# Depthwise-convolution images kept in device memory, and two pieces' results taken up behind the next scans

## The chip, the cores and the metric

The kernel runs on one core of one Trainium2 chip. The core has a matrix engine (TensorE, PE in the profile; its weight loads are listed apart as PEld), a vector engine (VectorE, DVE), a scalar engine (ScalarE, ACT), GpSimd (POOL) and SyncE (SP), which in this program does nothing but issue transfers. Each engine works through its own list of instructions in order, and waits on semaphores for the others. Sixteen DMA engines move what the queues hand them. The metric is device time in microseconds (us) of one execution, the median of several. All times here are microseconds unless another unit is named.

## What is computed

The program is a network of four layers on x of 4 images, 128 channels, 64×64 pixels. Only layers 0 and 1 are touched by the change. Cut to what matters, and with the group normalisation `_gn` over 32 groups of channels:

```python
x = x + conv_mamba(_gn(x), ...)     # layer 0
x = x + conv3x3(_gn(x), ...)        # layer 1, a full 3x3 convolution of 128 channels
# layers 2 and 3: attention and experts on the tokens (t = to_tokens(x)), not touched

def conv_mamba(x):                  # layer 0, for every image
    feat = gelu(dwconv2d(x, conv1_w, conv1_b))          # depthwise 3x3, zero padding
    ca = sigmoid(relu(feat.mean((2, 3)) @ ca1_w.T) @ ca2_w.T)
    feat = gelu(dwconv2d(feat * ca, conv2_w, conv2_b))  # depthwise 3x3
    scores = 0.7 * sigmoid(head(feat)) + 0.3 * sigmoid(10 * var_over_channels(x))
    order = argsort(-mean of scores over 4x4 patches)   # 256 patches are ranked
    x1n = layernorm(x in that order + pe in that order) # 4096 tokens of 128 channels
    xm, z = split(x1n @ in_proj_w.T)                    # 256 + 256
    xc = silu(conv1d(xm))                               # causal, 4 taps
    dt_low, B, C = split(xc @ x_proj_w.T)               # 8, 16, 16
    dt = softplus(dt_low @ dt_proj_w.T + dt_proj_b)
    # a scan over 4096 tokens, for 256 channels and 16 states
    h = exp(dt * A) * h + dt * B * xc ;  y = sum_s(h * C)
    y = (y + D * xc) * silu(z)
    return (y @ out_proj_w.T) put back by the inverse order
```

## The kernel before

Layers 0 and 1 are one function, `layers01` (from line 235). Its main loop is `scan` (line 544): the four images' sequences, 4096 tokens each, run one after the other in 8 chunks of 512 tokens, and each chunk in 8 groups of two states. A group has one product on VectorE (L683, `hs = dtx * b_ps`, 128×2048), four decays on ScalarE (L686, an Exp into PSUM, two buffers), four scans on VectorE (L687, `tensor_tensor_scan`), a copy of the last state (L690) and two products with C on GpSimd (L693), and eight matmuls on TensorE, one (`b_ps`, one PSUM buffer) that spreads B over the partitions for the next group and the rest (`y_ps`) that sums the states; `hs` has three buffers. There are 256 such groups. A chunk's inputs are prepared a step per group by the generator `enter` during the chunk before: xc, the gate z, dbc, dt, and then eight SP transfers (L624) that copy dt and dtx into the scan's layout (dt2, dtx2). The two rows of C are read back from a scratch array `c_d` in device memory, spread over partitions by two SP transfers per group (L656, `c_sb`, three buffers).

What else the layers need is done beside the scans, in pieces. `others(b)` is a generator of the work beside sequence b: `end(b-1)`, which puts the finished sequence back into its image, runs layer 1's convolution on it and stores it (`put_back`, `convolve`; the store is L755), and then `in_order(b+1)`, which prepares the next image: the load (L333), the group normalisation (`groupnorm_padded`: bn_stats at L135, the normalised and zero-padded image `xp` of 66×66 at L174), the two depthwise convolutions, the ranking, the permutation. Each `yield` of these generators names a cost; after every group the loop at the end of `scan` takes pieces until their costs reach what is due by then. What is due follows from COST_END, COST_ORDER and the table ROOM (a share for each group of a chunk). `in_order(0)` has no scans to run beside and runs alone at the start, and `end(3)` alone at the end.

A piece's matmuls are issued when it is taken; what takes their results up (an activation or a copy) is put in a list with `later(...)`, and `K.flush()` issues what the list holds. The loop flushes before every piece it takes:

```python
while done < due:
    K.flush()
    done += next(beside, due)
```

TensorE's order is the order in which this Python code issues (a manual schedule for PE alone). For the other engines' queues a scheduler sets the order by its own estimate of when each instruction can run. So an instruction that must wait can stand in a queue ahead of another that could go.

A depthwise convolution is done on TensorE: for each of 8 row blocks of the image, `gather` (L350 to L359) builds a tile `under` of 96 partitions, which are three row shifts of 32 channels, for each of the four channel groups; 12 matmuls (`convolved`, three column shifts by four groups; the trace counts 24) then make the convolution. `under` has two buffers. The source is the padded image in on-chip memory, xp for the first convolution and fp, the first one's gelu, for the second; a gather is 12 transfers of 66 KB, all issued by SP at L355. Per image there are 16 gathers, so 192 transfers.

Of the kernel before, what the change touches and what calls it, by code (L numbers as in the profile page):

```python
# [17 lines left out]
P = 128  # L18
NB = 4
HW = 64  # L20
# [9 lines left out]
class Common:  # L30
# [98 lines left out]
    def groupnorm_padded(self, xb, xp, small, psum):  # L129


        nc = self.nc
        st = small.tile([P, NCH, 6], F32, name="gn_st")
        for c in range(NCH):
            nc.vector.bn_stats(st[:, c, :], xb[:, c * CH : (c + 1) * CH])  # L135
            if c % 2:
                yield 1
        mv = small.tile([P, 2], F32, name="gn_mv")
        nc.vector.bn_aggr(mv, st)
        nc.gpsimd.memset(xp[:, 0, :], 0.0)  # L140
        nc.gpsimd.memset(xp[:, HW + 1, :], 0.0)
        nc.gpsimd.memset(xp[:, 1 : HW + 1, 0:1], 0.0)
        nc.gpsimd.memset(xp[:, 1 : HW + 1, HW + 1 : HW + 2], 0.0)
        yield 4
        mp = psum.tile([P, 1], F32, name="gn_mp", tag="mm")
        self.mm(mp, self.group_mean, mv[:, 0:1])
        gm = small.tile([P, 1], F32, name="gn_gm")
        v2 = small.tile([P, 1], F32, name="gn_v2")

        def variance():  # L150
            nc.vector.tensor_copy(gm, mp)
            d = small.tile([P, 1], F32, name="gn_d")
            nc.vector.tensor_tensor(d, mv[:, 0:1], gm, ALU.subtract)
            nc.vector.scalar_tensor_tensor(v2, d, d, mv[:, 1:2], ALU.mult, ALU.add)

        self.late.append(variance)
        yield 4
        yield 4
        vp = psum.tile([P, 1], F32, name="gn_vp", tag="mm")
        self.mm(vp, self.group_mean, v2)  # L160
        rs = small.tile([P, 1], F32, name="gn_rs")
        off = small.tile([P, 1], F32, name="gn_off")

        def scale():
            sd = small.tile([P, 1], F32, name="gn_sd")
            nc.scalar.activation(sd, vp, AF.Sqrt, bias=self.eps5)
            nc.vector.reciprocal(rs, sd)
            nc.vector.scalar_tensor_tensor(off, gm, -1.0, rs, ALU.mult, ALU.mult)

        self.late.append(scale)  # L170
        yield 4
        yield 4
        for c in range(NCH):
            nc.scalar.activation(  # L174
                xp[:, 1 + 8 * c : 9 + 8 * c, 1 : HW + 1],
                xb[:, c * CH : (c + 1) * CH].rearrange("p (y x) -> p y x", x=HW),
                AF.Identity,
                bias=off,
                scale=rs,
            )  # L180
            if c % 2:
                yield 1
# [52 lines left out]
def layers01(K, xd, dpool, w, w1):  # L235
# [4 lines left out]
    DS = 16  # L240
    NQ, NG = 4, DS // 2

    COST_END, COST_ORDER = 127.2, 215.2
    ROOM = (0.04, 0.04, 0.09, 0.21, 0.41, 0.61, 0.81, 1.0)
    with ExitStack() as ctx:
        pool = lambda name, bufs, **kw: ctx.enter_context(tc.tile_pool(name=name, bufs=bufs, **kw))
        cst = pool("l0_const", 1)
# [41 lines left out]
        spread = cst.tile([32, DS, 64], F32, name="spread")  # L289
        nc.vector.tensor_copy(spread, state.unsqueeze(2).to_broadcast([32, DS, 64]))  # L290
        c_d = dpool.tile([2, DS, CH], F32, name="c_d")

        pair = cst.tile([P, 64], F32, name="pair")
        nc.vector.tensor_tensor(pair, K.ident[:, 0:64], K.ident[:, 64:128], ALU.add)
# [41 lines left out]
        def in_order(b, made, work, psum):  # L336
# [10 lines left out]
            nc.gpsimd.memset(fp[:, 1 : HW + 1, HW + 1 : HW + 2], 0.0)  # L347
            fsum = small.tile([P, NCH], F32, name="fsum")

            def gather(img, c):  # L350

                t = work.tile([96, 4, 8 * (HW + 2)], F32, name="under", bufs=2)
                for ky in range(3):
                    for g in range(4):
                        nc.sync.dma_start(  # L355
                            out=t[32 * ky : 32 * ky + 32, g],
                            in_=img[32 * g : 32 * g + 32, 8 * c + ky : 8 * c + ky + 8, :].rearrange("p y x -> p (y x)"),
                        )
                return t  # L359

            def convolved(under, taps):
# [10 lines left out]
                        )  # L372
                return ps

            under = gather(xp, 0)
            yield 4
            unders = [under, gather(xp, 1)]
            for c in range(NCH):
                ps = convolved(unders.pop(0), deep1)
                later(  # L380
                    nc.scalar.activation,
                    fp[:, 1 + 8 * c : 9 + 8 * c, 1 : HW + 1],
                    ps.rearrange("p (y x) -> p y x", x=HW),
                    AF.Gelu,
                    bias=conv1_b,
                    accum_out=fsum[:, c : c + 1],
                )
                if c + 2 < NCH:
                    unders.append(gather(xp, c + 2))
                yield 5  # L390
            favg = small.tile([P, 1], F32, name="favg")
            nc.vector.tensor_reduce(favg, fsum, AX.X, ALU.add)
            nc.vector.tensor_scalar(favg, favg, 1.0 / L, None, ALU.mult)
            unders = [gather(fp, 0), gather(fp, 1)]
            yield 4
            c1p = psum.tile([32, 1], F32, name="c1p", tag="mm")
            mm(c1p, ca1_wT, favg)
            c1 = small.tile([32, 1], F32, name="c1")
            later(nc.scalar.activation, c1, c1p, AF.Relu)
            yield 4  # L400
            c2p = psum.tile([P, 1], F32, name="c2p", tag="mm")
            mm(c2p, ca2_wT, c1)
            ca = small.tile([P, 1], F32, name="ca")
            later(nc.scalar.activation, ca, c2p, AF.Sigmoid)
            yield 2

            sm = small.tile([P, 256], F32, name="sm")
            for c in range(NCH):  # L410
# [8 lines left out]
                f2 = work.tile([P, CH], F32, name="f2", tag="ln_xc")  # L419
                later(nc.scalar.activation, f2, ps, AF.Gelu, bias=conv2_b, scale=ca)  # L420
                if c + 2 < NCH:
                    unders.append(gather(fp, c + 2))
                yield 5
                vp = psum.tile([P, CH], F32, name="pv_var", tag="mm")
                mm(vp, K.var1, sq)
                pv = work.tile([P, CH], F32, name="pv")
                later(nc.scalar.activation, pv, vp, AF.Tanh, scale=5.0)
                yield 1.2
                hp = psum.tile([P, CH], F32, name="head", tag="mm")
                mm(hp, head_bc, f2)  # L430
                sc = work.tile([P, CH], F32, name="sc")
                later(nc.scalar.activation, sc, hp, AF.Tanh, bias=head_b, scale=0.5)
                yield 1.2
                nc.vector.scalar_tensor_tensor(sc, pv, 3.0 / 7.0, sc, ALU.mult, ALU.add)
                nc.vector.tensor_reduce(
                    sm[:, 32 * c : 32 * c + 32].rearrange("p (a b) -> p a b", b=16),
# [45 lines left out]
            for c in range(NCH):  # L482
# [14 lines left out]
                later(nc.scalar.activation, sq, mp, AF.Square)  # L497
                later(nc.scalar.copy, xl, mp)
                yield 1.2
                vp = psum.tile([P, CH], F32, name="pos_var", tag="mm")  # L500
                mm(vp, K.mean, sq)

# [9 lines left out]

                K.late.append(normed)
                yield 1.2
                for a in range(2):
                    nc.scalar.activation(
                        xn[:, :, 16 * (2 * c + a) : 16 * (2 * c + a) + 16].rearrange("p (y x) b -> p y b x", x=4),
                        xl[:, a * 256 : (a + 1) * 256].rearrange("p (y b x) -> p y b x", y=4, x=4),
                        AF.Identity,
                        bias=norm_b,  # L520
                        scale=norm_g,
                    )
# [6 lines left out]
            for o in range(0, 16, 2):  # L529
                tp = psum.tile([P, 4, P], F32, name="perm_t", tag="mm")  # L530
                for j in range(4):
                    h = j % 2
                    nc.tensor.transpose(tp[:, j, :], xn[:, o + j // 2, h * P : (h + 1) * P], K.ident)
                ts = work.tile([P, 4, P], F32, name="perm_s", tag="pv")
                later(nc.vector.tensor_copy, ts, tp)
                yield 1.2
                pp = psum.tile([P, 2, 256], F32, name="perm_p", tag="mm")
# [3 lines left out]
                yield 2.2  # L541
            made.append((xq, perm_inv))

        def scan(seqs, others, work, psum, psbc, psex, psy):
# [127 lines left out]
            for n, (b, c) in enumerate(chunks):  # L672
# [7 lines left out]
                for g in range(NG):  # L680
# [24 lines left out]
                    if g > 0:  # L705
                        next(leaving, None)
                    next(coming, None)
                    while done < due:
                        K.flush()
                        done += next(beside, due)  # L710
                    if past is not None:
                        add(*past)
                        if g == 0:
                            leaving = leave(past[0])
                            next(leaving)
# [6 lines left out]
        def put_back(xb, om, perm_inv, prep, psum):  # L722
# [3 lines left out]
            for o in range(0, 16, 2):  # L726
# [4 lines left out]
                ts = prep.tile([P, 4, P], F32, name="perm_s", tag="pv")  # L731
                later(nc.scalar.copy, ts, tp)
                yield 1.2
                pp = psum.tile([P, 2, 256], F32, name="perm_p", tag="mm")
                for j in range(4):
                    mm(pp[:, j // 2, :], ts[:, j, :], perm_inv[j % 2], start=j % 2 == 0, stop=j % 2 == 1)
                for j in range(2):
# [3 lines left out]
                        nc.vector.tensor_tensor, at, at, pp[:, j, :].rearrange("p (a b) -> p a b", b=16), ALU.add  # L741
                    )
                yield 2.2

        def convolve(b, xb, psum):

# [2 lines left out]
            for c in range(2 * NCH):  # L749
# [2 lines left out]
                at = xb[:, c * CH // 2 : (c + 1) * CH // 2]  # L752
                later(nc.vector.scalar_tensor_tensor, at, ps, bias, at, ALU.add, ALU.add)
                yield 4.5
            nc.sync.dma_start(out=xd[b], in_=xb)  # L755

        def end(b, seq, work, psum):
# [1001 lines left out]
```

## Time and profile before

| | us |
|---|---|
| median of 3 runs | 10960.34 (10960.1 to 10969.78) |
| the profiled execution, its own time | 10954.31 |
| its span in the trace | 10952.5 |
| stage 1, `in_order(0)` alone | 0 to 276 |
| scans of sequences 0 to 3, with the work beside them | 276 to 3069 |
| `end(3)` alone | 3069 to 3250 |
| layers 2 and 3 | 3250 to 10952 |

Times of the eight chunks of the scans, from the starts of the products of L683 (a chunk is eight groups; the last chunk of sequence 3 is counted to the start of its last group):

| sequence | chunks 0 to 7, us |
|---|---|
| 0 | 67.7, 92.9, 85.9, 78.7, 79.9, 105.7, 89.6, 72.6 |
| 1 | 90.1, 82.0, 105.5, 95.7, 90.2, 84.3, 143.0, 80.3 |
| 2 | 90.3, 81.9, 105.7, 95.2, 87.7, 84.1, 142.8, 79.9 |
| 3 | 75.9, 75.8, 80.1, 71.5, 69.1, 69.7, 69.5, 47.1 |

How it is read. A page of the profile has the busy time of each engine, and groups of instructions by line and operation: how many, their busy time, the mean of one, and the idle time of the engine just before them with what ended it. A line of the waits view reads "engine, what waited <- what released it: total us, times, longest". A line of a timeline reads "start, us, engine, line, operation, output<-input, shapes, count, [idle before <- releaser]". SPq is SP's queue of issues; the time of such a line is the time of issuing, not of moving the data. Idle time of an engine that the rest does not wait for costs nothing, so an engine's share of busy time alone does not say what a change is worth. A line such as L328 or L90 is that of a helper (`later` and `mm`), and the tile's name says which step it is.

### The profile page before, as it was taken

Reading aid. Unit: us, or ns where it says so; the run is one execution under the profiler, and the core shown is the slowest. Engines: PE = TensorE matmul, PEld = TensorE weight load, DVE = VectorE, ACT = ScalarE, POOL = GpSimd, SP = SyncE. Lnnn points to the kernel's source line nnn. Section 1 sums busy time; section 2 is a strip of 40 time slices with the busy share of each in tenths; the row PEclk is TensorE's granted clock in tenths of the full one; section 3 lists DMA queues with packets and bytes.
Section 4 is the critical chain, followed back from the end, with each engine's and each line's share of the span. In section 5 each row is a group of like instructions: output and inputs, shape, how many; then the busy total and the mean of one; then the engine's idle time right before and its main releaser. Section 6 shows DMA issues by size and latency. Waiting matters only on the chain. (4 is left out here: it accounts for less than half of the span.)

```text
span 10952.5 us, 184078 instructions
## 1 busy us (share of the span) xinstructions
PE 9041.6 (83%) x71952; PEld 3464.4 (32%) x71952; DVE 7656.5 (70%) x8462; ACT 7514.8 (69%) x10319; POOL 5233.6 (48%) x3143
## 2 busy tenths in 40 slices
PE   5777778777857999968999968999969999966767
PEld 2223323222332333323333323333323333323333
DVE  2788668668846777757777757777757777744563
ACT  2666565665527999958999948999948999932431
POOL 1565555556624666535665535665535655620000
PEclk8788878877878999979999979999979999977888
DMA  3322322322212222121221222212222212123004
GB/s 83 87 67 57 90 69 56 99 59 59 70 52 40 38 32 34 32 78 35 37 33 33 32 78 38 33 34 33 32 79 39 33 33 34 30 88 96 14 16 139
DMA packets 524327, 581.59 MB, mean 53 GB/s; under 512 B 106233, under 2 KB 329537, under 8 KB 520897
## 3 DMA queue, kind: packets, MB, share of 16 engines
q1 hardware_dynamic: 523456, 569.81, 22.6%
q8 instruction: 568, 9.31, 0.4%
q14 instruction: 303, 2.47, 0.1%
HBM read 373.96 MB, written 76.55 MB: 41 GB/s over the span
## 5 line engine op out<-in xcount | busy, mean ns | idle before, releaser
L1204 ACT ACTIVATE ex<-score 128x1024 f32<-128x1024 f32 x5120 | 4932.2, 1032 | 471.0 <-PE score L90 180.8
L90 PE MATMUL ctx_ps<-ex,qt 128*32 128x512 f32 x20480 | 2719.1, 595 | 0.0
L1151 POOL TENSOR_TENSOR folded<-ex 128x1024 f32<-128x1024 f32 x704 | 1679.4, 2386 | 2073.6 <-ACT ex L1204 2062.0
L1210 DVE STREAM_TRANSPOSE turned<-ex 128x1024 f32<-128x1024 f32 x1536 | 1879.5, 1224 | 470.1 <-ACT ex L1204 426.9
L90 PE MATMUL acc_ps<-turned,turned_v 128*32 128x256 f32 x24576 | 1826.3, 388 | 180.2 <-DVE turned L1190 177.4
L1190 DVE STREAM_TRANSPOSE turned<-ex 128x1024 f32<-128x1024 f32 x1536 | 1854.0, 1207 | 0.0
L90 PE MATMUL score<-queries,keys 32*128 32x512 f32 x10240 | 1359.9, 496 | 120.5 <-ACT ex L1204 74.3
L687 DVE TENSOR_TENSOR_SCAN hs<-decay,carry,hs 128x512 f32<-128x512 f32 x1024 | 1253.0, 1266 | 200.3 <-ACT decay L686 186.0
L686 ACT ACTIVATE decay<-dt,a_neg 128x512 f32<-128x512 f32 x1024 | 701.0, 689 | 788.0 <-DVE hs L687 764.3
L693 POOL TENSOR_TENSOR hs<-hs,c_sb 128x1024 f32<-128x1024 f32 x512 | 1204.9, 2374 | 46.1 <-DMA c_sb<-c_d 26.7
L90 PEld LDWEIGHTS score<-queries,keys 32*128 32x128 f32 x10240 | 524.7, 182 | 2176.5 <-issue 1664.1
L1152 POOL TENSOR_TENSOR quarters<-folded 128x512 f32<-128x512 f32 x704 | 905.1, 1286 | 55.2
L90 PEld LDWEIGHTS acc_ps<-turned,turned_v 128*32 128x32 f32 x24576 | 562.1, 108 | 897.0 <-issue 556.0
L90 PEld LDWEIGHTS ctx_ps<-ex,qt 128*32 128x32 f32 x20480 | 684.0, 110 | 461.0 <-DVE ctx L1133 53.2
L683 DVE TENSOR_TENSOR hs<-dtx,b_ps 128x2048 f32<-128x2048 f32 x256 | 582.2, 2274 | 256.6 <-PE b_ps L90 173.4
L90 PE MATMUL y_ps<-hs,pair 128*64 128x512 f32 x2048 | 644.2, 752 | 137.3 <-POOL hs L693 137.2
L1133 DVE COPY ctx<-ctx_ps 128x512 f32<-128x512 f32 x256 | 177.0, 691 | 669.6 <-PE ctx_ps L90 663.2
L690 POOL COPY carry<-hs 128x4 f32<-128x4 f32 x256 | 59.3, 232 | 1019.7 <-DVE hs L687 976.8
L1023 POOL TENSOR_TENSOR turned_v<-v,quarter 128x1024 f32<-128x1024 f32 x192 | 459.2, 2392 | 18.1 <-DMA v<-value_d 18.1
L1197 DVE TENSOR_REDUCE dacc<-quarters 128x2 f32<-128x512 f32 x704 | 453.4, 644 | 8.0 <-POOL quarters L1152 8.0
L90 PE MATMUL ln_var<-ln_sq,mean 128*128 128x512 f32 x384 | 240.2, 710 | 182.9 <-ACT ln_sq L105 158.1
L90 PE MATMUL b_ps<-dbc,spread 32*128 32x512 f32 x512 | 319.4, 706 | 70.7 <-DVE hs L683 70.7
(353 smaller groups left out, 9684.3 us busy)
## 6 DMA issues: line engine op xcount, KB each, us to landing
c_sb<-c_d SPq DMA_DIRECT2D x512, 128.0 KB
queries<-head_d SPq DMA_DIRECT2D x1024, 64.0 KB
keys<-head_d SPq DMA_DIRECT2D x1024, 64.0 KB
dt<-dt SPq DMA_DIRECT2D x128, 256.0 KB
dtx<-dtx SPq DMA_DIRECT2D x128, 256.0 KB
w<-in_L_ffn_weight SPq DMA_DIRECT2D x32, 1024.0 KB
w<-in_L_ffn_weight SPq DMA_DIRECT2D x128, 256.0 KB
under<-xp SPq DMA_DIRECT2D x384, 66.0 KB
```

The source lines that it names most:

```text
L90: self.nc.tensor.matmul(out, lhsT, rhs, start=start, stop=stop)
L683: nc.vector.tensor_tensor(hs, dtx2, bb.unsqueeze(1).to_broadcast([P, NQ, CH]), ALU.mult)
L686: nc.scalar.activation(ex, dt2[:, q, :], AF.Exp, scale=a_neg[:, q, g : g + 1])
L687: nc.vector.tensor_tensor_scan(hs[:, q, :], ex, hs[:, q, :], carry[:, g, q : q + 1], ALU.mult, ALU.add)
L693: nc.gpsimd.tensor_tensor(at, at, cs.unsqueeze(1).to_broadcast([P, 2, CH]), ALU.mult)
L1023: nc.gpsimd.tensor_tensor(t, v.unsqueeze(2).to_broadcast([P, 4 * BT, 4, HD]), quarter.unsqueeze(1).to_broadcast([P, 4 * BT, 4, HD]), ALU.mult,
L1151: nc.gpsimd.tensor_tensor(hs, exs[:, :, 0], exs[:, :, 1], ALU.add)
L1152: nc.gpsimd.tensor_tensor(qs, hs[:, :, 0 : CH // 2], hs[:, :, CH // 2 :], ALU.add)
L1190: nc.vector.transpose(*upright)
L1197: nc.vector.tensor_reduce(at, qs, AX.X, ALU.add)
L1204: nc.scalar.activation(ex, sps[p], AF.Exp, scale=scale, accum_out=dacc[:, j, h, t : t + 1] if summed else None)
L1210: nc.vector.transpose(*upright)
```

## The change

Three things are done together.

1. A padded image `image_d` (128×66×66) is kept in device memory. `give` writes to it, by transfers that ScalarE issues: the whole normalised image once per image (2.2 MB), and each of the first convolution's eight row blocks behind its gelu (270 KB). `gather` reads from it with three transfers per block, one per row shift, of 270 KB each, instead of twelve from on-chip memory. Per image that is 48 gathers and 9 gives, 57 transfers, where there were 192. The second block of a convolution is gathered together with the first one, in one piece.
2. The loop keeps the results of up to two pieces in the list before it flushes, so that they can land behind the next group's scans. Where a piece needs the results of the one before, the generators now flush themselves.
3. The pieces are cut and paced otherwise: a yield of 8 between the image's load and its bn_stats, a yield of 4 behind the first gathers, COST_END 135.2 for 127.2, COST_ORDER 227.2 for 215.2, and another table ROOM.

```diff
     def groupnorm_padded(self, xb, xp, small, psum):
         st = small.tile([P, NCH, 6], F32, name="gn_st")
+        yield 8
         for c in range(NCH):
             nc.vector.bn_stats(st[:, c, :], xb[:, c * CH : (c + 1) * CH])
...
         self.late.append(variance)
         yield 4
+        self.flush()
         yield 4
...
-    COST_END, COST_ORDER = 127.2, 215.2
-    ROOM = (0.04, 0.04, 0.09, 0.21, 0.41, 0.61, 0.81, 1.0)
+    COST_END, COST_ORDER = 135.2, 227.2
+    ROOM = (0.05, 0.05, 0.12, 0.26, 0.44, 0.63, 0.81, 1.0)
...
         c_d = dpool.tile([2, DS, CH], F32, name="c_d")
+        image_d = dpool.tile([P, HW + 2, HW + 2], F32, name="image_d")
...
-            def gather(img, c):
+            def give(img, at, n):
+
+                nc.scalar.dma_start(out=image_d[:, at : at + n, :], in_=img[:, at : at + n, :])
+
+            def gather(c):
 
                 t = work.tile([96, 4, 8 * (HW + 2)], F32, name="under", bufs=2)
                 for ky in range(3):
-                    for g in range(4):
-                        nc.sync.dma_start(
-                            out=t[32 * ky : 32 * ky + 32, g],
-                            in_=img[32 * g : 32 * g + 32, 8 * c + ky : 8 * c + ky + 8, :].rearrange("p y x -> p (y x)"),
-                        )
+                    nc.sync.dma_start(
+                        out=t[32 * ky : 32 * ky + 32],
+                        in_=image_d[:, 8 * c + ky : 8 * c + ky + 8, :].rearrange("(g p) y x -> p g (y x)", g=4),
+                    )
                 return t
...
-            under = gather(xp, 0)
+            give(xp, 0, HW + 2)
             yield 4
-            unders = [under, gather(xp, 1)]
+            unders = [gather(0), gather(1)]
+            yield 4
             for c in range(NCH):
                 ps = convolved(unders.pop(0), deep1)
                 later(
...
                     accum_out=fsum[:, c : c + 1],
                 )
+                later(give, fp, 1 + 8 * c, 8)
                 if c + 2 < NCH:
-                    unders.append(gather(xp, c + 2))
+                    unders.append(gather(c + 2))
                 yield 5
+            K.flush()
...
-            unders = [gather(fp, 0), gather(fp, 1)]
             yield 4
+            unders = [gather(0), gather(1)]
...
                 if c + 2 < NCH:
-                    unders.append(gather(fp, c + 2))
+                    unders.append(gather(c + 2))
                 yield 5
+                K.flush()
...
+                    held = 0
                     while done < due:
-                        K.flush()
+                        if held == 2:
+                            K.flush()
+                            held = 0
                         done += next(beside, due)
+                        held += 1
```

The flushes that are left out here stand in the same way ahead of the step that needs a result: in the group normalisation, the channel attention, the scores of a block, the layer norm, the permutation, `put_back` and ahead of the store in `convolve`.

More of the change, by code (lines that the diff above doesn't have):

```diff
@@ L171, in groupnorm_padded @@
         yield 4
+        self.flush()
         yield 4
@@ L421, in in_order @@
                 if c + 2 < NCH:
-                    unders.append(gather(fp, c + 2))
+                    unders.append(gather(c + 2))
                 yield 5
+                K.flush()
                 vp = psum.tile([P, CH], F32, name="pv_var", tag="mm")
@@ L428, in in_order @@
                 yield 1.2
+                K.flush()
                 hp = psum.tile([P, CH], F32, name="head", tag="mm")
@@ L433, in in_order @@
                 yield 1.2
+                K.flush()
                 nc.vector.scalar_tensor_tensor(sc, pv, 3.0 / 7.0, sc, ALU.mult, ALU.add)
@@ L499, in in_order @@
                 yield 1.2
+                K.flush()
                 vp = psum.tile([P, CH], F32, name="pos_var", tag="mm")
@@ L514, in in_order @@
                 yield 1.2
+                K.flush()
                 for a in range(2):
@@ L536, in in_order @@
                 yield 1.2
+                K.flush()
                 pp = psum.tile([P, 2, 256], F32, name="perm_p", tag="mm")
@@ L541, in in_order @@
                 yield 2.2
+            K.flush()
             made.append((xq, perm_inv))
@@ L707, in scan @@
                     next(coming, None)
+                    held = 0
                     while done < due:
-                        K.flush()
+                        if held == 2:
+                            K.flush()
+                            held = 0
                         done += next(beside, due)
+                        held += 1
                     if past is not None:
@@ L733, in put_back @@
                 yield 1.2
+                K.flush()
                 pp = psum.tile([P, 2, 256], F32, name="perm_p", tag="mm")
@@ L743, in put_back @@
                 yield 2.2
+            K.flush()
         def convolve(b, xb, psum):
@@ L754, in convolve @@
                 yield 4.5
+            K.flush()
             nc.sync.dma_start(out=xd[b], in_=xb)
```

## The prediction

> **What bounds the kernel now.** I read the page first, then windows by stage, the waits of DVE and PE, and last the timelines around the longest waits. The windows (columns: span of the stretch, busy time and count of PE, PEld, DVE, ACT, POOL, granted TensorE clock, DMA share, GB/s), stage 1 and then the scans of sequences 0 to 3:
>
> ```profile
> 0.00:276.00 276.00, 161.34 (x598) 63.13 (x598) 56.53 (x135) 81.64 (x127) 28.98 (x40) 0.86 0.33 84
> 276.00:949.00 673.00, 506.54 (x1442) 151.61 (x1442) 530.32 (x422) 435.02 (x568) 400.29 (x238) 0.80 0.30 75
> 949.00:1720.00 771.00, 588.33 (x1856) 232.05 (x1856) 552.97 (x483) 447.24 (x586) 410.87 (x254) 0.83 0.28 72
> 1720.00:2488.00 768.00, 583.27 (x1856) 230.83 (x1856) 553.08 (x482) 447.08 (x586) 410.96 (x254) 0.84 0.28 72
> 2488.00:3069.00 581.00, 464.21 (x1280) 172.97 (x1280) 499.33 (x399) 319.83 (x422) 392.55 (x232) 0.83 0.24 64
> ```
>
> The change lies in the first 3250 us; from there on both programs issue the same instructions in the same order (PE 38157, ACT 6416, DVE 6576 of them), so 7700 us count as unchanged. In the scans no engine is full: PE and DVE, the fullest, are 588 and 553 of 771 us busy beside sequence 1 (76 and 72%). A group needs 7.3 us of DVE (one product 2.27, four scans 1.26) and takes 8.7 us in sequence 3's later chunks, with little beside it; sequences 1 and 2 average 12 (771/64 and 768/64). The time is therefore in waits of DVE, and those say of what:
>
> ```profile
> DVE hs L687 <- ACT decay L686: 186.0, 110, 7.6
> DVE hs L683 <- PE b_ps L90: 173.4, 86, 7.8
> DVE hs L683 <- DMA dtx<-dtx: 67.6, 5, 17.5
> DVE gn_st L135 <- DMA xb<-in_x: 28.8, 2, 14.5
> ```
>
> (total, times, longest). The last two can be placed. One dtx wait, and one load wait:
>
> ```profile
> 1299.13 15.11 SPq L355 DMA_DIRECT2D under<-xp  x24
> 1314.34 1.18 SPq L656 DMA_DIRECT2D c_sb<-c_d  x2
> 1315.56 3.19 SPq L624 DMA_DIRECT2D dt<-dt  x4
> 1318.86 3.58 SPq L624 DMA_DIRECT2D dtx<-dtx  x4
> ```
> ```profile
> 1202.08 4.81 DVE L687 TENSOR_TENSOR_SCAN hs<-decay,carry,hs 128x512 f32<-128x512 f32 x4
> 1221.21 4.84 DVE L135 BATCH_NORM_STATS2 gn_st<-xb 128x6 f32<-128x512 f32 x8 [14.32 <-DMA xb<-in_x]
> 1232.03 2.29 DVE L683 TENSOR_TENSOR hs<-dtx,b_ps 128x2048 f32<-128x2048 f32 x1 [4.29 <-PE b_ps L90]
> 1327.69 2.29 DVE L683 TENSOR_TENSOR hs<-dtx,b_ps 128x2048 f32<-128x2048 f32 x1 [17.30 <-DMA dtx<-dtx]
> ```
>
> SP spends 15.11 us issuing 24 gather transfers, 0.63 each, and the dt and dtx copies of the next chunk stand behind them: DVE idles 17.30 us for them. And DVE's queue holds bn_stats ahead of the next product, so the scan stands 14.32 us for an image load that it does not need.
>
> Stage 1 has the same queue without cover. PE waits for `under` 24.3 us in 8 waits, and conv1's gelus end 7.86 us apart (from 49.87 to 104.89, seven periods), which is the issue time of 12 transfers (24.47 us for 38, 0.64 each: 7.7):
>
> ```profile
> 35.82 24.47 SPq L355 DMA_DIRECT2D under<-xp  x38
> PE conv L90 <- DMA under<-xp: 24.3, 8, 8.8
> ```
>
> **The change part by part.** The sum is made against the profiled execution, 10954.3 us (span 10952.5, 1.8 around it), which is 6.0 below the median of 10960.3.
>
> *Stage 1.* Lost: conv1's first gather must wait until all eight xp activations are done (ACT's xp row ends at 40.7; before, the first rows sufficed) and the 2.2 MB store has landed. The nearest rows are loads of 2.1 MB: issued 19.05, used 27.05 (8.0 us), and 1212.42 to 1221.21 (8.8). I take 8.4, then 5 for a gather: 1.9 to issue three, some 3 to land (the c_sb pair issued from 1297.86 was read by POOL at 1301.71: 3.85, issue included). Conv1 starts at 54, not 43: +11. Gained: a period becomes (5 + 4.86)/2 = 4.93, two buffers, 4.86 being PE's mean for one conv in this stage (77.7 us busy/16); seven periods, −20.5. Were PE's 5.79 of conv1 itself (46.3 us over 8) the floor, −14.5. Conv2 is paced by PE and ACT (period 7.66 with 12 issues hidden in it): 0. Net −9.5; between −18 (store 5 us: xd's 2.1 MB moved from 1200.7 to 1206) and +6 (gathers from device memory at 8 us).
>
> *Image 1, beside sequence 0.* One dtx wait of 13.51 us ends at 441.96, behind conv1's gathers. A gather is now 3 issues, 1.9 us for 7.6, so the copies come 10 to 15 us sooner. The give stands three groups (22 us of DVE) ahead of its conv in the built PE order, which covers 13.4. SP waits for that store too, with one c_sb pair of the next group behind it; c_sb has three buffers, and POOL's work is not what DVE waits for: 0. −14; between −25 (two b_ps waits of 4.4 and 4.7 go too) and 0 (PE or ACT is late next).
>
> *Images 2 and 3, beside sequences 1 and 2; places of the first.* (a) A new yield puts bn_stats behind 12 scans, 15 us, and the load (8.8) has landed: from 1192.2 (group 6 of chunk 2) to group 1 of chunk 3, 44.6 us become 22 of DVE for three groups, 5.7 of bn work, 4.3 of the b_ps wait at 1232: 32, −12.6. What is late next is the groupnorm's chain, which now runs inside chunk 3. (b) There ACT gets a lump in one group: 6 table loads at 1.28, four decays, two xc, the softplus and half the xp activations, 21 us against 7.3; and then the new wait: conv1's first conv stands in PE's hand-written order ahead of b_ps of the group after. Store 8.4, gather 5, conv 4.9, b_ps 1.3: 19.7, less the 5 that DVE still has in hand: 14.7. Groups 1 to 6 took 51.4, and become five groups: 21 + 7.3×2 + 14.7 + 16.8 (two groups with carried-over pieces) = 67.1: +15.7. (c) Then come the groups that stood behind the gathers (15.0, 24.5 and 12.5 = 52, the dtx wait in them): PE's two convs 7.4, b_ps 1.3, y 2.6 and 1.7 of others give 13 each, 39: −13. (d) ACT's queue: 9 gives at some 0.5 to issue (single transfers on SP took 0.35 to 0.54) stand ahead of decays; half of 4.5 shows, +2. (e) SP's queue: three of the four dtx copies for chunk 4 are built behind the fifth gather, whose buffer the third conv frees; that conv is done before group 7's b_ps, 13 us ahead of their product, and gather, copies and landing take 1.9 + 1.9 + 5.3 (last dtx issue 1322.4 to 1327.7) = 9: 0, and +2 to +9 if the groups run at 7.3. POOL's four memsets of xp and of fp move with the chain, 0: POOL is 411 of 771 us busy. Net −8 each, −16 for two. Bounds: (b) hidden wholly, −23 each; (c) giving nothing, +5 each; with (e) at its worst +14.
>
> *Holding two results.* The inner flushes keep every dependent step in place, and the built orders differ little: PE's matmul count is the same, ACT has two table loads fewer (386 for 388, −2.6 of ACT). 0; ±10 for all sequences, from the decay wait's 186 us: a twentieth either way. *New pacing (yields of 8 and 4, ROOM):* moves end(b−1) earlier within a chunk; 0 to −2, taken as 0. *Sequence 3 and end(3):* no image is made there: 0.
>
> Sum −9.5 − 14 − 16 = −39.5: 10914.8, and on the median's scale 10921; say **10920**.
>
> **A rule against it.** In conv1 of stage 1 (35 to 106 us) SP issues without a break while the DMA engines' share is 0.42. The Trainium skill, "DMA: Bandwidth & Descriptors", section "Issuing engines are not separate DMA queues", says that the time to initiate a DMA is "usually small relative to the DMA itself"; on that reading fewer issues save nothing, only the trip through device memory would be left, and my sum would be +11 in stage 1 and −12.6 + 15.7 + 2 for each of images 2 and 3: +21 (10981 on the median's scale). The rows of this trace decide otherwise: the issue of 66 KB transfers paces the conv. The same page's section "Anatomy of one DMA" (a fit on the software path) gives 2.0 us plus bytes over 436e3: as an estimate 7.1 for the whole give and 3.9 for a gather, 11.0 for my 13.4; no run here shows that fit, and it would move the sum by −2.4 in three places.
>
> **The rivals.**
> *ACT's queue is held (slower).* Each piece's give stands in ACT's order with a wait: it overwrites rows that the gather of the next chunk reads, so it may go only when that has landed, and the decays behind it wait too. For: 186 us of DVE's waits are for decays already. Against: that gather was issued a conv earlier, some 5 to 13 us before. 24 piece gives and 3 whole ones lie in the scans. At 4.5 us each, near the whole latency of a gather: 27×4.5 = 122, less the 2×2 already counted: −40 + 118 = +78, 11038 by the median. It decides from (40 + 22)/27 = 2.3 us per give.
> *Nothing comes of it (same).* SP's issue goes, but DVE then waits at the same places for PE or ACT: b_ps waits (173 us, 86 times) show PE as near behind. Image 1 gives 0, (c) gives nothing, stage 1 its −9.5: 10954.3 − 9.5 + 2×5 = 10954.8, 10961 by the median.
> *The new wait is covered (faster).* Three hs buffers let DVE and POOL run ahead, and (b)'s 14.7 goes for two images: −29 more, about 10891. Against: b_ps has one buffer, and it is b_ps that stands behind the conv.
>
> **How the numbers follow.** Forecast (10900 to 10938) 0.44; wait covered 0.14; same 0.19; ACT held, or another slower case (conv1 in stage 1 no faster and (b) as worked out), 0.23. Some 0.2%, 22 us, is what a measurement of this kernel can tell from no change. Faster by more than that (below 10938): the forecast's 0.44 less a margin of 0.01, and the covered case's 0.14: 0.57. Same (10938 to 10982): that 0.01 and 0.18 of the second rival, 0.19. Slower: ACT's 0.23 and 0.01 of the second rival, 0.24. The range must reach through the same case and into part of ACT's case, and down through the covered case: 10870 to 11005, with 0.05 left out below and 0.14 above. The forecast's own range is 10900 to 10938.
>
> **What the profile after should show.** SP: gathers in threes per chunk, 1.9 us; no dtx wait of 13 to 17 us; bn_stats without a wait for xb. Stage 1: conv1's start near 54 and gelus 4.9 apart. Images 2 and 3: one PE wait for `under` near 13 us each and, behind it, a product waiting some 15 for b_ps; a group of 20 us or more ahead of it. ACT: gives of 0.5 us without long waits behind them. Wrong it would be made by decay waits growing well over 186 us (ACT's queue held), by gathers from device memory that land later than 8 us, or by b_ps waits that take all that the dtx waits leave.

## The result and the profile after

The changed kernel takes 10984.83 us (median of 20 runs, 10962.57 to 10999.45) where before takes 10962.19 (20 runs, 10944.97 to 10977.47): a ratio of 1.0017, with a 95% interval of 1.0010 to 1.0024. It is some 19 us slower. The forecast was 40 us faster: the time lies inside the range, on the wrong side of no change.

The two profiled executions lie further apart than that, 10989.47 and 10954.31. Cut by the starts of the products (the product of a group is L683 before and L702 after), the spans differ so:

| stretch | before | after | difference | forecast |
|---|---|---|---|---|
| stage 1, to the first product | 281.3 | 256.3 | −25.0 | −9.5 |
| sequence 0 (image 1 beside it) | 673.2 | 679.1 | +5.9 | −14 |
| sequence 1 (end 0, image 2) | 771.0 | 785.4 | +14.4 | −8 |
| sequence 2 (end 1, image 3) | 767.8 | 784.5 | +16.7 | −8 |
| sequence 3 (end 2, no image), to its last product | 558.6 | 569.9 | +11.3 | 0 |
| from there to the end | 7900.6 | 7912.3 | +11.7 | 0 |

The last line holds end(3) and layers 2 and 3. In the runs below it is anywhere between 7888 and 7919, so nothing is read from it. Without it the two traces differ by 23.4, close to what the medians say. Stage 1 gained two and a half times what was forecast. The scans gave back 48 us, and not only where images are made: sequence 3 makes none and lost 11.

By chunks the loss has a few places:

| | chunks 0 to 7, after (before in the table above) |
|---|---|
| 0 | 66.3, 85.0, 77.0, 84.3, 90.9, 95.8, 105.4, 74.4 |
| 1 | 91.5, 81.4, 82.0, 121.2, 91.6, 84.8, 154.9, 77.9 |
| 2 | 91.4, 81.3, 82.0, 120.3, 92.0, 85.0, 154.8, 77.7 |
| 3 | 79.3, 78.1, 73.4, 73.8, 72.5, 71.3, 70.7, 50.9 |

In sequences 1 and 2, chunk 2 lost its load wait (105.5 to 82.0), chunk 3 grew by 25.5 and chunk 6 by 12. The waits of DVE in the scans, changed kernel:

```profile
DVE hs L702 <- PE b_ps L90: 250.5, 99, 23.8
DVE hs L706 <- ACT decay L705: 182.9, 98, 6.8
DVE hs L702 <- DMA dtx<-dtx: 31.0, 2, 17.1
DVE gn_st L136 <- DMA xb<-in_x: 0.6, 1, 0.6
```

The waits for transfers went for the most part: the dtx waits are 31.0 for 67.6, 17.1 of it at the very first product, and the load's 28.8 are 0.6. The waits for b_ps took their place, 250.5 for 173.4. The decay wait did not grow (182.9 for 186.0), so ACT's queue was not held by the gives. One wait of each of sequences 1 and 2 is the one that the prediction worked out as (b). Timelines of ACT, SP, PE and DVE, changed kernel, image 2:

```profile
1260.13 0.33 ACTq L356 DMA_DIRECT2D image_d<-xp  x1
1263.42 2.05 SPq L643 DMA_DIRECT2D dt<-dt  x2
...
1270.45 1.13 SPq L675 DMA_DIRECT2D c_sb<-c_d  x2
1271.62 1.31 SPq L643 DMA_DIRECT2D dt<-dt  x2
1273.04 0.63 SPq L643 DMA_DIRECT2D dtx<-dtx  x1
1273.77 29.35 SPq L362 DMA_DIRECT2D under<-image_d  x15
...
1281.56 5.35 PE L90 MATMUL conv<-under,deep 96*32 96x512 f32 x24 [29.67 <-DMA under<-image_d]
1286.83 2.07 PE L90 MATMUL b_ps<-dbc,spread 32*128 32x512 f32 x2
...
1289.01 2.29 DVE L702 TENSOR_TENSOR hs<-dtx,b_ps 128x2048 f32<-128x2048 f32 x1 [23.45 <-PE b_ps L90]
```

The give is issued at 1260.13 and the first gather only at 1273.77, though the store's data had moved by 1266.5. The first gather stood in SP's order behind a c_sb pair and copies of dt and dtx, which had POOL to wait for. No wait of SP for the store itself is among its waits from 1255 to 1312; the two for POOL are:

```profile
SPq L643 <- POOL carry L709: 11.9, 1, 11.9
SPq L675 <- POOL carry L709: 5.4, 1, 5.4
```

From the gather's issue to the conv it is 7.8 us, with the copies just issued ahead of it. So DVE waited 23.45 us, not 14.7.

Stage 1, where PE waits for the first gather and ACT takes up the second convolution, changed kernel:

```profile
53.50 7.83 PE L90 MATMUL conv<-under,deep 96*32 96x512 f32 x48 [19.02 <-DMA under<-image_d]
```
```profile
111.22 0.78 ACT L332 ACTIVATE f<-conv,conv_b,ca 128x512 f32<-128x512 f32 x1 [2.15 <-PE conv L90]
116.88 0.78 ACT L332 ACTIVATE f<-conv,conv_b,ca 128x512 f32<-128x512 f32 x1 [2.15 <-PE conv L90]
122.54 0.78 ACT L332 ACTIVATE f<-conv,conv_b,ca 128x512 f32<-128x512 f32 x1 [2.15 <-PE conv L90]
```

and the same activations before:

```profile
123.45 0.78 ACT L328 ACTIVATE f<-conv,conv_b,ca 128x512 f32<-128x512 f32 x1 [2.12 <-PE conv L90]
131.11 0.78 ACT L328 ACTIVATE f<-conv,conv_b,ca 128x512 f32<-128x512 f32 x1 [2.17 <-PE conv L90]
```

Conv1 starts at 53.5 (54 was forecast). Its gelus run from 58.82 to 95.72, 5.27 apart (4.93 forecast), and end 9.2 earlier than before. Then conv2, which was to change by nothing, has a period of 5.65 instead of 7.66: seven periods, another 14 us. Where that comes from is taken up with the run of twelve transfers.

### The profile page after: what moved, and what is told of

Its sections match the earlier page's. It is cut to its first block, busy times and chain, and to the rows that moved or that the text cites. A ratio compares the mean times of both kernels' runs of the same rounds, so it can differ in the third digit from the quotient of the medians.

```text
span 10987.6 us, 183426 instructions
## 1 busy us (share of the span) xinstructions
PE 9016.1 (82%) x71952; PEld 3453.7 (31%) x71952; DVE 7671.4 (70%) x8462; ACT 7513.2 (68%) x10317; POOL 5238.2 (48%) x3143
## 5 line engine op out<-in xcount | busy, mean ns | idle before, releaser
L706 DVE TENSOR_TENSOR_SCAN hs<-decay,carry,hs 128x512 f32<-128x512 f32 x1024 | 1251.0, 1266 | 196.9 <-ACT decay L705 182.9
L702 DVE TENSOR_TENSOR hs<-dtx,b_ps 128x2048 f32<-128x2048 f32 x256 | 582.7, 2276 | 292.0 <-PE b_ps L90 250.5
L90 PE MATMUL ln_var<-ln_sq,mean 128*128 128x512 f32 x384 | 247.6, 731 | 187.4 <-ACT ln_sq L105 164.0
```

The costliest lines, as they stand in the source:

```text
L90: self.nc.tensor.matmul(out, lhsT, rhs, start=start, stop=stop)
L702: nc.vector.tensor_tensor(hs, dtx2, bb.unsqueeze(1).to_broadcast([P, NQ, CH]), ALU.mult)
L706: nc.vector.tensor_tensor_scan(hs[:, q, :], ex, hs[:, q, :], carry[:, g, q : q + 1], ALU.mult, ALU.add)
```

## The experiments

The change has three parts: the images, the holding of two results, and the pacing (two yields, the costs, ROOM). The first runs make one part at a time. All kernels compute the whole of the reference. Ratios are against before in the same series, with 95% intervals.

**One part at a time.** *Holding alone:* before, with the `held` loop and the inner flushes.

```diff
+                    held = 0
                     while done < due:
-                        K.flush()
+                        if held == 2:
+                            K.flush()
+                            held = 0
                         done += next(beside, due)
+                        held += 1
```

> Before with the held results and the inner flushes alone: no images in device memory, the old pacing. Theory A (what cost the time in sequence 3, +11 us where no image is made, is the holding of two results): stage 1 unchanged at 281 us, sequence 3's scans 8 to 12 us longer than before's, sequences 1 and 2 some 5 to 12 each, whole program +15 to +30. Theory B (it is the new pacing): every sequence within 2 us of before, whole program within 5.

Measured: 10951.47 (11 runs), ratio 0.9998 (0.9989 to 1.0006); sequence 3 at 562.3. Holding neither costs nor brings anything that can be measured.

*Pacing alone:* before, with the new yields, costs and ROOM, every piece flushed.

```diff
+        yield 8
         for c in range(NCH):
             nc.vector.bn_stats(...)
...
-    COST_END, COST_ORDER = 127.2, 215.2
-    ROOM = (0.04, 0.04, 0.09, 0.21, 0.41, 0.61, 0.81, 1.0)
+    COST_END, COST_ORDER = 135.2, 227.2
+    ROOM = (0.05, 0.05, 0.12, 0.26, 0.44, 0.63, 0.81, 1.0)
...
             unders = [under, gather(xp, 1)]
+            yield 4
```

> Before with the new yields, costs and table alone (the inner flushes are there and change nothing, since every piece is flushed): no images, no holding. Theory A: the load's wait of 14 us goes in sequences 1 and 2 (chunk 2 some 20 us shorter), chunk 3 gives part of it back behind 12 issues for a gather, sequence 3 within 3 us of before: whole program -10 to -25. Theory B: sequence 3 +8 to +12, chunk 6 of sequences 1 and 2 +12 each, whole program +10 to +30.

Measured: 10986.07 (5 runs), ratio 1.0035 (1.0023 to 1.0048), some 38 us. Sequence 3 takes 569.7, chunk 6 takes 156.6 and 154.8, chunks 4 and 6 of sequence 0 take 90.5 and 103.4: the changed kernel's own losses, without an image in device memory. The whole goes as theory B said, and somewhat beyond its range. Chunk 2 shows the load wait gone (82.2 and 82.0), as theory A said, but that gain is paid for elsewhere: in chunk 6, in sequence 3, and in chunk 3 (109.2 and 108.3 for 95.7 and 95.2), which so makes about half of its growth without the new wait.

*Images alone:* the changed kernel with the old pacing and a flush per piece.

> Images in device memory alone, with the old pacing and every piece flushed. If the images cost nothing beside the scans (theory A): stage 1 -25 as in the changed kernel, sequences 1 to 3 within 5 us of before, whole program -25 to -40. Rival C (the round trip through device memory itself costs 15 us and more in each of sequences 1 and 2, wherever the pieces lie): stage 1 -25, sequences 1 and 2 +15 each, whole program 0 to +10.

Measured: 10931.93 (11 runs), ratio 0.9979 (0.9970 to 0.9988), 23 us faster than before. Stage 1 ends at 256.2, the sequences take 672.4, 774.4, 774.6 and 558.6. Theory A, with 3 and 7 us of loss beside sequences 1 and 2. The three parts add up: −0.21, −0.02 and +0.35% make +0.12, and +0.17 was measured.

**The pacing taken apart.** *ROOM alone, and yields with costs alone,* each in before:

> Before with the new table ROOM alone. Theory D (the table puts pieces earlier in a chunk, into groups whose own steps are full): the whole loss of the pacing run, +25 to +45, with sequence 3's scans some 8 to 12 longer and chunk 6 of sequences 1 and 2 10 to 14 longer. Theory E (the new yields and costs move the pieces): within 6 us of before.

> Before with the new yields and costs, and the old table. Theory D: within 6 us of before beside sequence 3, and -10 to -25 beside sequences 1 and 2, where the load's wait of 14 us goes. Theory E: +25 to +45.

Measured: 10956.65, ratio 0.9994 (0.9985 to 1.0003), and 10961.89, ratio 1.0006 (0.9997 to 1.0015). Both theories fell: neither alone costs anything that can be told, and together they cost 38 us. What they do together is seen in chunk 6, where the position pieces lie (a matmul, a Square on ACT, then a `pos_var` matmul on its result). Times from one product to the next, groups 3 to 6: before 19.9, 26.2, 21.4, 25.6; ROOM alone 21.6, 27.3, 27.4, 17.8; yields alone 14.3, 24.9, 22.6, 33.5; the changed kernel 13.1, 41.0, 25.2, 23.7. By the costs handed out, group 3 takes two of these rounds in each of the others, and three in the kernels with both; the traces show as many `pos_var` steps in PE's order between the b_ps of groups 4 and 5, in sequence 1 as in 2. All of them stand ahead of the b_ps that the product of group 5 needs, and that is also the stretch in which ACT makes the next chunk's dt. Three rounds alone are not the price: the stretch behind it has three in all of these kernels and takes 21 to 28. The two long waits for `ln_sq` in that stretch in the changed kernel, and then the one of before:

```profile
1560.64 2.08 PE L90 MATMUL pos_var<-ln_sq,mean 128*128 128x512 f32 x2 [11.31 <-ACT ln_sq L332]
1578.36 2.07 PE L90 MATMUL pos_var<-ln_sq,mean 128*128 128x512 f32 x2 [12.31 <-ACT ln_sq L332]
```
```profile
1582.58 2.08 PE L90 MATMUL pos_var<-ln_sq,mean 128*128 128x512 f32 x2 [9.35 <-ACT ln_sq L328]
```

PE stands still for ACT twice, and the scans behind it. ACT in turn waits there for GpSimd's last step of a round (`xl`, L527): 5.15, 3.52 and 4.76 us, ahead of the next round's Square in its queue. *The changed kernel with the old ROOM:*

```diff
-    ROOM = (0.05, 0.05, 0.12, 0.26, 0.44, 0.63, 0.81, 1.0)
+    ROOM = (0.04, 0.04, 0.09, 0.21, 0.41, 0.61, 0.81, 1.0)
```

> The changed kernel with the old table ROOM put back, nothing else. Theory F (the table and the yields each cost nothing alone, but together they put three position pieces into the one group of chunk 6 that also makes the next chunk's dt): chunk 6 of sequences 1 and 2 at 139 to 143 for 155, whole program 25 to 40 below the changed kernel, 10945 to 10960. If the table is not what makes the difference: 10985, chunk 6 at 155.

Measured: 10947.54 (11 runs), ratio 0.9983 (0.9975 to 0.9992). Chunk 6 takes 135.3 and 144.2. One table turns the changed kernel from 0.17% slower into 0.17% faster, theory F. That chunk is 30 us of it in the trace's two sequences (309.7 to 279.5). Why sequences 0 and 3 lose by the pacing was not taken apart; in the traces ROOM alone costs sequence 3 some 8 us (566.5) and the yields alone 4 (563.0), which both gain elsewhere.

*Images and holding, old pacing:*

> The changed kernel with the old pacing: images and held results. If the parts add up, 10930, within 6 us of the run with images alone, since holding two results alone moved nothing; if holding helps the images' gives, 5 to 10 less.

Measured: 10935.82 (11 runs), ratio 0.9983 (0.9974 to 0.9992): the parts add up.

**What the images gain by.** *Twelve transfers from device memory:*

```diff
                 for ky in range(3):
-                    nc.sync.dma_start(out=t[32 * ky : 32 * ky + 32], in_=image_d[...three axes...])
+                    for g in range(4):
+                        nc.sync.dma_start(out=t[32 * ky : 32 * ky + 32, g], in_=image_d[32 * g : 32 * g + 32, ...])
```

> The run with images alone, but each gather in twelve transfers of 66 KB from device memory instead of three of 270 KB. If the number of issues is what paced the first convolution (theory A): its gelus come 7.6 to 8 us apart again, stage 1 ends some 25 to 40 us later than with three transfers, whole program +5 to +20 against before. If it was the source of the reads: gelus near 5 us apart, and the time of the run with images alone (10932).

Measured: 10995.42 (5 runs), ratio 1.0036 (1.0024 to 1.0049): 63 us above the run with three transfers, from which it differs in nothing but the count. With the same number of transfers the way through device memory loses 0.36%; it is the count that gains. Stage 1 ends at 290.7, 34.5 later. Conv1's gelus come in pairs, 14.6 us from pair to pair (60.02, 73.82, 88.63, 103.88), so 7.3 per conv, and PE waits 33.4 us for `under`, 18.8 of it for the first gather.

Conv2 has before's period to the hundredth:

```profile
133.20 0.78 ACT L331 ACTIVATE f<-conv,conv_b,ca 128x512 f32<-128x512 f32 x1 [3.11 <-PE conv L90]
140.86 0.78 ACT L331 ACTIVATE f<-conv,conv_b,ca 128x512 f32<-128x512 f32 x1 [2.17 <-PE conv L90]
```

Twelve issues at before's 0.64 would be 7.7, but that is not what sets it. From device memory an issue takes 0.46 (24 in 11.00 us from 47.69), and SP, done with twelve in 5.4 us, then waits for PE. The waits of SP's queue in conv2 of this run (130 to 175), and those of PE for conv2's gelu (0 to 300):

```profile
SPq L362 <- PE conv L90: 15.8, 5, 8.1
PE head L90 <- ACT f L331: 8.7, 8, 2.2
```

From conv2's second block on PE's matmuls wait for ACT's gelu alone and for no transfer (two weight loads wait 0.76 each), and the same holds for conv2 of before. What differs is PE's order. Before, and then the changed kernel:

```profile
133.86 1.05 PE L90 MATMUL conv<-under,deep 96*32 96x512 f32 x4
134.84 1.12 PE L90 MATMUL pv_var<-ln_sq,var 128*128 128x512 f32 x2
135.90 2.77 PE L90 MATMUL conv<-under,deep 96*32 96x512 f32 x20
```
```profile
119.62 2.79 PE L90 MATMUL conv<-under,deep 96*32 96x512 f32 x24
122.34 1.13 PE L90 MATMUL pv_var<-ln_sq,var 128*128 128x512 f32 x2
```

With twelve transfers, from either source, the scores' `pv_var` splits the convolution in two, and the gelu comes 2 us later in every block; with three, the convolution is whole and `pv_var` covers the gelu. The manual schedule of PE holds for the scans alone (the `with` block around `scan`); stage 1 is built outside it, so there the scheduler orders PE too, and it built another order for another count of transfers. Conv2's 14 us are the gain of that order, not of the issues that SP saves.

For conv1 of before the issues do set the pace: SP issues without a break at 0.63 (prediction), and PE waits for `under`. The Trainium skill's sentence that the time to initiate is "usually small relative to the DMA itself" ("DMA: Bandwidth & Descriptors", "Issuing engines are not separate DMA queues") does not hold for these 66 KB transfers: at 0.63 us each the DMA engines were busy for 0.42 of the time, and PE waited 24.3 us.

*Device memory for the first image alone:*

```diff
-            give(xp, 0, HW + 2)
...
+            if b == 0:
+                give(xp, 0, HW + 2)
```

> Device memory for the first image alone, where nothing runs beside; images 1 to 3 as before, old pacing, every piece flushed. If the whole gain of the images is in stage 1 (theory A): stage 1 -25, the sequences as before, 3 to 10 less in sequences 1 and 2 than the run with images alone: 10922 to 10935. If the images help the scans too: 10936 to 10950.

Measured: 10937.91 (11 runs), ratio 0.9980 (0.9971 to 0.9989); stage 1 257.7, scans 2770.0 us for before's 2770.5 and 2780.1 with all images. So the images' whole gain is stage 1's, as theory A had it. The time itself lies 3 us above theory A's range: the 10 us by which the scans are shorter than with all images in the trace do not show in the ratios (0.9980 and 0.9979).

**The new wait.** *The give in four:* each part right behind two of the eight normalising activations, in the changed kernel.

```diff
     def groupnorm_padded(self, xb, xp, small, psum, give=None):
...
+            if c % 2 and give is not None:
+                give(xp, 0 if c == 1 else 8 * c - 7, 16 if 1 < c < NCH - 1 else 17)
             if c % 2:
                 yield 1
...
-            give(xp, 0, HW + 2)
```

> The changed kernel with the whole image's give split into four, each right behind two of the eight normalising activations. Theory G (the wait of 23.5 us ahead of the first convolution of images 2 and 3 is the store and what SP has to issue first): the wait falls to 5 to 12 us, stage 1 is 3 to 6 shorter, whole program 20 to 35 below the changed kernel. If PE's order makes the wait whatever the store does: within 6 us of the changed kernel.

Measured: 10932.28 (6 runs), ratio 0.9970 (0.9957 to 0.9982). PE's wait for the first gather of image 2 goes from 29.67 to 4.68:

```profile
1245.16 5.35 PE L90 MATMUL conv<-under,deep 96*32 96x512 f32 x24 [4.68 <-DMA under<-image_d]
1250.44 2.07 PE L90 MATMUL b_ps<-dbc,spread 32*128 32x512 f32 x2
```

Chunk 3 goes from 121.2 to 105.3, and SP now issues the first gathers ahead of the copies; for the copies behind them DVE waits 12.19 us again. Theory G; the gain, some 50 us by the ratios, is more than expected, and 37.5 of it stand in the scans of the trace. The edit did two things at once, the earlier store and another order of SP's queue, and no run parts them.

*The same with images alone:*

> The run with images alone (10932) with the give split in the same way. Theory G: the group of 25.7 us in chunk 3 of sequences 1 and 2 falls to 14 to 18, stage 1 is 3 to 6 shorter: 10905 to 10925. Otherwise 10932.

Measured: 10901.15 (5 runs, 10897.14 to 10908.60), ratio 0.9945 (0.9932 to 0.9957). Chunk 3 takes 87.9 for 99.4, stage 1 ends at 247.6, 8.6 sooner. Of the 37 us that the ratios give over the run with images alone, the traces show 24.5 up to the last product; the rest lies behind the scans, where the two kernels do not differ. This kernel beats both: 0.55% faster than before, 0.7% than the change.

*Gives issued by GpSimd:* the last kernel with one word changed.

```diff
-                nc.scalar.dma_start(out=image_d[:, at : at + n, :], in_=img[:, at : at + n, :])
+                nc.gpsimd.dma_start(out=image_d[:, at : at + n, :], in_=img[:, at : at + n, :])
```

> The run with images alone and the give split (10901), with the gives issued by GpSimd instead of ScalarE. Theory H (SP's copies of dt and dtx, and its c_sb pairs, wait for gives to land, 31 and 18 us in that run, because a transfer takes up a completion semaphore that an earlier give of the same kind of queue still holds; a give from GpSimd holds another): SP's waits for image_d go, the dtx wait of 14 us beside sequence 0 goes, and 10 to 30 us come off: 10870 to 10890. Against it: GpSimd's queue must then wait for the gelus, with the products with C behind them: 10900 to 10940. If the waits for gives hide other waits that end as late: 10895 to 10905.

The reason for it is a wait of SP in the scans of the run before it, the kernel with the split give:

```profile
SPq L642 <- DMA image_d<-fp: 30.9, 5, 8.8
SPq L674 <- DMA image_d<-fp: 18.4, 4, 5.6
```

L642 copies dt and dtx and L674 reads c_d: neither touches the image. With the gives on GpSimd these waits are gone, and two waits of gathers for parts of xp's give (58.6 us together) have come. The dtx wait beside sequence 0, 13.9 us in the changed kernel and 14.1 with images alone, falls from 14.22 us (split give) to 1.62 (GpSimd):

```profile
408.70 2.29 DVE L701 TENSOR_TENSOR hs<-dtx,b_ps 128x2048 f32<-128x2048 f32 x1 [14.22 <-DMA dtx<-dtx]
```
```profile
401.61 2.29 DVE L701 TENSOR_TENSOR hs<-dtx,b_ps 128x2048 f32<-128x2048 f32 x1 [1.62 <-DMA dtx<-dtx]
```

The scans of its trace are 25.5 us shorter (2738.7 for 2764.2), stage 1 is 3.7 longer. Yet the time is 10899.35 (5 runs, 10893.26 to 10909.15), ratio 0.9951 (0.9937 to 0.9964), no better than the kernel before it. Most of the 25.5 lies in sequences 1 and 2 (12.6 and 10.2); sequence 0 loses in chunk 2 most of what it gains in chunk 1 (84.4 to 91.6, 91.9 to 81.5). So theory H's mechanism is shown, and its worth stays open: the two were timed in different series, and the part behind the scans was 11 us longer in this trace.

## Why the prediction was wrong

- *New pacing, "0 to −2, taken as 0".* This is the step that failed, and the sign of the forecast with it. Alone it costs 0.35%, 38 us. With (a), which also comes from a new yield, the forecast had the pacing at −25. What (a) promised came, chunk 2 lost 23 in each of sequences 1 and 2 of the pacing run, but chunk 3 took back 13 in each, chunk 6 14 and 12, and sequence 3 11. I priced yields and table by the cost they shift, and did not follow which pieces then fall into which group. The costs can be handed out on paper in both versions, and that shows three rounds of PE and ACT for two in group 3 of chunk 6.
- *The images without (a).* The forecast comes to −14.3 for them, and the trace with images alone shows −15.5 up to the last product. That the two agree is luck: stage 1 gained 15.5 more than forecast, and image 1 13 less.
- *Stage 1, −9.5.* Conv1 was right in its start (53.5 for 54) and its sum (−9.2); its parts, +9.0 to the first gelu and −18.1 over seven periods, were each some 2 smaller than forecast. The term "conv2: 0" was wrong by 14 us. That PE and ACT pace it was right, and the run with twelve transfers shows it; what was missed is that the scheduler would build PE's order anew in this stage. The lower bound of −18 does not follow from a store of 5 us, which gives −12.9, and the measured −25 lies outside the bounds.
- *Image 1, −14.* The dtx wait was 13.51 before and is 13.9 after. That shorter issuing would bring the copies forward was wrong: SP waits for PE to free `under`, and its copies wait for gives to land, which the GpSimd run removed. What sequence 0 gained in chunks 1 and 2 (178.8 to 162.0) came with the pacing run too (165.0).
- *Images 2 and 3.* (a) was right in kind: chunk 2 lost 23.5 us, where 12.6 were forecast with a part of the next. (b) was right as a mechanism and too small, 23.45 for 14.7; the store was faster than taken (some 6 for 8.4), and what I left out were 7 us of SP's queue, a c_sb pair waiting for POOL and five copies, between store and gather. I had looked at SP's order for the copies behind the gathers, not for those ahead. (c) to (e): chunks 2 to 4 took 294.8 for 291.4, where −8 was forecast.
- *Holding two results, 0.* Right, 0.9998.
- *The rivals.* ACT's queue was not held: its decay waits fell by 3 us. The new wait was not covered. The slower side came by a way that none of the rivals named.

## What to carry to other kernels

Hand the pieces out on paper before pricing a change of pacing: one more round between two engines, in a group that is already full, cost more than the transfers saved. A period that equals a number of issues times the time of one need not come from them: look for the wait that ends it, and compare the built orders. A large store that a load needs is worth cutting into parts that follow their producers: here four parts instead of one took the images' gain from 23 to 60 us by the ratios (15.5 to 39.9 in the traces, up to the last product).

## What the hardware showed

- The whole image, 2.2 MB, left at 429 GB/s and had moved some 6.3 us after its issue; loads of 2.1 MB took 8.0 to 8.8. Rate in slices of 0.65 us from 1258, changed kernel:

```profile
GB/s 0 0 0 0 429 429 429 429 429 429 429 429 85 224 224 274 0 0 0 0 0 139 233 230 199 274 243 243 203 221 205 201 205 250 218 244 211 202 224 159
```

- Issuing a 66 KB transfer took SP 0.64 us from on-chip memory (38 in 24.47, before) and 0.46 from device memory (24 in 11.00, the run with twelve), one of 264 KB from device memory 0.45 (6 in 2.69 from 47.67, changed kernel).
- A transfer of SP can wait for one that ScalarE issued and that has nothing to do with its data. In the traces the transfers of SP and ScalarE carry the same eight completion semaphores (101 to 108) in turn, and a transfer waits until the one that carried its semaphore before has landed: with the split give, a give of 396.31 and a copy of dtx both carry 108, and the copy, after a wait of 6.2 for it, is issued at 402.61. GpSimd's gives carry eight others (111 to 118). So a give that waits for a gelu holds back copies eight places on.
- Layers 2 and 3, with the same instructions in the same order, took up to 30 us more in one execution than in another (7888 to 7919 with end(3)), more than most differences here; in before and the runs with holding alone and with the first image alone the scans of sequences 1 and 2 repeat within 4 us (771.0 to 773.5, and 767.8 to 771.2).
